# Attention and mixture of experts in one kernel: each put of rows waits for the one two in front of it

## The chip, the cores and the metric

The kernel runs on one core of a Trainium2 chip. The metric is the device time of one execution in microseconds (us); the time of the kernel before is the median of three executions. Beside these there is one profiled execution, from which all the timelines, waits and chains in this document come. PE is the matrix engine, DVE the vector engine, ACT the scalar engine, POOL the GpSimd engine; SP is the engine that issues most DMA transfers.

## The reference

The input is 16 sequences of 256 tokens with 128 channels, in float32. Four residual blocks follow each other; each one normalises its input first.

```python
x = x + attn_a(layernorm(x))   # 16 heads of 8, softmax inside blocks of 64 tokens of a sequence
x = x + ffn(layernorm(x))
x = x + attn_b(layernorm(x))   # over the axis of 16 sequences, 16 heads of 8, with a fixed bias
x = x + ffn(layernorm(x))      # the same weights as the first ffn

def ffn(x):                    # 4096 tokens, 8 experts, hidden size 512
    logits = x @ Wr
    top_vals, top_idx = top_k(logits, 2)
    rw = softmax(top_vals)
    combine = sum(rw[..., None] * one_hot(top_idx, 8), axis=1)
    h = silu(einsum('nc,ech->neh', x, Wg)) * einsum('nc,ech->neh', x, Wu)
    eo = einsum('neh,ehc->nec', h, Wd) / sqrt(12)
    return einsum('ne,nec->nc', combine, eo)
```

Each token needs only its two chosen experts, so the kernel computes only those: 8192 pairs of token and expert.

## The kernel before

The tokens are cut into four quarters `q` of 1024 tokens (64 positions of every sequence), and a quarter is held in SBUF as `xq[q]`, eight groups `g` of 128 tokens. There are two layers, `layer` 0 (attention a, then experts) and `layer` 1 (attention b, then experts).

**Attention.** `attention_a` (L397) and `attention_b` (L487) are generators that go through half a quarter in steps. In attention a, POOL adds each group's result to `xq` (L449, read here as the attention add). `layernorm_t` (L266) uses POOL for the power -1/2 (L279, the tiles `rs`), and `add_row` (L309) adds a bias row on POOL.

**Routing.** `router(layer, q)` (L585) normalises a quarter, computes the logits on PE, picks two experts for every token on DVE, and works out for each pair the row of a large table in DRAM, `sorted_in[layer]`, in which the rows of each expert lie together. It then puts the rows there: for each of the 8 groups and both choices one indirect DMA on POOL's queue (L694) takes 128 rows of 132 numbers from the tile `row` and writes each to its own place `pos_i`. That is 16 puts for a quarter, 128 in both layers. Each has to follow a DVE instruction named `beat`, the last of the attention or expert step issued beside it. The tile `row` is one of two buffers; a copy (L605) into it marks its next use.

**Experts.** `experts(layer)` (L852) goes through 39 tiles of 256 sorted rows. Which tile belongs to which expert is read from tables that `tile_tables` (L710) computes on DVE in three lists of 9, 8 and 22 tiles: the first list may start when the rows of two quarters are in place, the second after the third quarter, the last after the fourth. `fetch` (L853) issues four DMAs on SP's queue: the tile's rows `xin` (L861), which has to wait for all puts of rows that its list knows of, and the expert's three weights (L877 to L879). There are three buffers for each, so a tile is fetched two tiles ahead. PE turns the rows (`xt`, L889), computes `g` and `u` (L947) and, through `th` and `h` on ACT and DVE, `acc` (L897) and the turned result `y` (L908); ACT weighs it into `yo` (L913), DVE computes the places `to` (L918), and POOL puts the 256 result rows by two indirect DMAs (L920) into `results[layer]`: 156 puts in both layers. `y` and `to` have six buffers each.

**Combining.** `combine` (L969) reads result rows back on SP's queue (L973), after all puts of those tiles that may hold them (`READY`), and adds them to `xq`. In layer 1 the sum goes out.

**What sets the order.** The loops at the end weave generators: routing of one quarter and units of expert tiles run beside the attention of the next quarter. The Tile framework then schedules instructions on each engine's queue by its own estimate of when each can start, and sets semaphore waits for the dependences. [...] Puts into one table don't order each other, because they are declared members of a group without dependences:

```python
tc.declare_no_dep(put_row.ins, group=key, reason="rows of different places")
tc.add_to_no_dep_group(key, put_row.ins)
follow(put_row.ins, before[layer] + beat)
```

`follow` adds a dependence by hand. The framework gives the DMAs on POOL's queue eight completion semaphores in turn, so a put waits for the one eight in front of it before.

Of the kernel before, what the change touches and what calls it, by code (L numbers as in the profile page):

```python
# [110 lines left out]
def hybrid_kernel(  # L111
# [19 lines left out]
    nc = tc.nc  # L131
# [85 lines left out]
    rows = [const.tile([P, NG, TOP, RW], F32, name=f"rows{i}") for i in range(2)]  # L217
# [8 lines left out]
    sorted_in = [dram.tile([NE * NTOK, RW], F32, name=f"sorted_in{i}") for i in range(2)]  # L226
    results = [dram.tile([TOP * NTOK + KMAX * TT, C], F32, name=f"results{i}") for i in range(2)]
# [15 lines left out]
    before, after, puts = {}, {}, {}  # L243
# [3 lines left out]
    def follow(ins, others):  # L247
        for other in others:
            tc.add_manual_dep(ins, other.name, SYNC, reason="rows by places read at run time")
# [2 lines left out]

    beat, att_last = [None], [None]
    arrived = [None]


    def behind_now(put):
# [327 lines left out]
    def router(layer, q):  # L585
        n = f"F{layer}_{q}"
        row = rows[q % 2]
# [88 lines left out]
        place = p1.tile([P, NG, NE], F32, tag="place", name=f"place_{n}")  # L676
# [14 lines left out]
        key = f"rows_{layer}"  # L691
        for g in range(NG):
            for k in range(TOP):
                put_row = nc.gpsimd.indirect_dma_start(  # L694
                    out=sorted_in[layer],
                    out_offset=bass.IndirectOffsetOnAxis(ap=pos_i[:, k, g : g + 1], axis=0),
                    in_=row[:, g, k, :], in_offset=None,
                )
                tc.declare_no_dep(put_row.ins, group=key, reason="rows of different places")
                tc.add_to_no_dep_group(key, put_row.ins)  # L700
                follow(put_row.ins, before[layer] + beat)
                after.setdefault((layer, q), []).append(put_row.ins)
                yield
            if next(listing, listing) is None:
                yield
# [146 lines left out]
    def experts(layer):  # L852
        def fetch(li, i):  # L853
            n = f"{layer}_{li}_{i}"
            t = p3.tile([P, 2, RW], F32, tag="xin", name=f"xin_{n}")
            tab_i, behind = tables[layer, li]
            row = nc.values_load(
                tab_i[0:1, 1, i : i + 1], engines=[SP], min_val=0, max_val=NE * NTOK - TT,
                skip_runtime_bounds_check_because="no tile is behind the last expert's region",
            )  # L860
            got = nc.sync.dma_start(  # L861
                out=t.rearrange("p b r -> p (b r)"),
                in_=sorted_in[layer][bass.ds(row, TT)].rearrange("(p b) r -> p (b r)", b=2),
            )
            known = [put for q in range(LISTED + li) for put in after[layer, q]]
            key = f"rows_{layer}"
            tc.declare_no_dep(
                got.ins, group=key, keep=known, reason="rows that the list did not know"
            )
            tc.add_to_no_dep_group(key, got.ins)  # L870
            follow(got.ins, known)
            e = nc.values_load(
                tab_i[0:1, 0, i : i + 1], engines=[SP], min_val=0, max_val=NE - 1,
                skip_runtime_bounds_check_because="a count of at most NE - 1 experts",
            )
            w = p3.tile([P, 3, HID], F32, tag="w", name=f"w_{n}")
            nc.sync.dma_start(out=w[:, 0], in_=wg[bass.ds(e, 1)].rearrange("e c h -> (e c) h"))  # L877
            nc.sync.dma_start(out=w[:, 1], in_=wu[bass.ds(e, 1)].rearrange("e c h -> (e c) h"))
            nc.sync.dma_start(  # L879
                out=w[:, 2].rearrange("p (n c) -> p n c", c=C),  # L880
                in_=wd[bass.ds(e, 1)].rearrange("e (n p) c -> p (e n) c", p=P),
            )
            return t, w, no_pads if behind is None else behind[:, i]

        def turned(li, i, t):
            s = f"{layer}_{li}"
            pt = psum(f"xt_{s}_{i}")
            for b in range(2):
                nc.tensor.transpose(pt[:, b * P : (b + 1) * P], t[:, b, 0:C], ident)  # L889
            xT = p2.tile([P, TT], F32, tag="xT", name=f"xT_{s}_{i}")  # L890
            nc.scalar.copy(xT, pt[:, 0:TT])
            return xT

        def down(li, i, t, w, elsewhere, acc, pair, h):
            for j in range(2):
                hc = 2 * pair + j
                nc.tensor.matmul(  # L897
                    acc[:, 0:TT], lhsT=w[:, 2, hc * P : (hc + 1) * P],
                    rhs=h[:, j * TT : (j + 1) * TT],
                    start=(hc == 0), stop=(hc == NHC - 1),  # L900
                )
            if pair == 1:
                n = f"{layer}_{li}_{i}"
                yT = p2.tile([P, TT], F32, tag="yT", name=f"yT_{n}")
                nc.scalar.copy(yT, acc[:, 0:TT])  # L905
                py = psum(f"y_{n}")
                for b in range(2):
                    nc.tensor.transpose(  # L908
                        py[:, b * P : (b + 1) * P], yT[:, b * P : (b + 1) * P], ident
                    )  # L910
                y = p6.tile([P, 2, C], F32, tag="y", name=f"yo_{n}")
                for b in range(2):
                    nc.scalar.activation(  # L913
                        y[:, b, :], py[:, b * P : (b + 1) * P], AF.Identity,
                        scale=t[:, b, C : C + 1],
                    )
                to = p6.tile([P, 2], I32, tag="to", name=f"to_{n}")
                nc.vector.tensor_tensor(to, t[:, :, C + 1], elsewhere, ALU.max)  # L918
                for b in range(2):
                    put_row = nc.gpsimd.indirect_dma_start(  # L920
                        out=results[layer],
                        out_offset=bass.IndirectOffsetOnAxis(
                            ap=to[:, b : b + 1], axis=0
                        ),
                        in_=y[:, b, :], in_offset=None,
                    )
                    key = f"result_{layer}"
                    tc.declare_no_dep(put_row.ins, group=key, reason="rows of different places")
                    tc.add_to_no_dep_group(key, put_row.ins)
                    puts.setdefault(layer, []).append(put_row.ins)  # L930

        todo = [(li, i) for li, k in enumerate(LISTS) for i in range(k)]
        fetched = [fetch(*todo[0]), fetch(*todo[1])]
        xT = turned(*todo[0], fetched[0][0])
        pending = None
        for at, (li, i) in enumerate(todo):
            t, w, elsewhere = fetched.pop(0)
            s = f"{layer}_{li}"
            acc = ps_acc.tile([P, 512], F32, tag="acc", name=f"acc_{s}_{i}")
            for pair in range(2):  # L940
                m = f"{s}_{i}_{pair}"
                pg = ps_gu.tile([P, CH], F32, tag="gu", name=f"g_{m}")
                pu = ps_gu.tile([P, CH], F32, tag="gu", name=f"u_{m}")
                for k, p in ((0, pg), (1, pu)):
                    for j in range(2):
                        hs = slice((2 * pair + j) * P, (2 * pair + j + 1) * P)
                        nc.tensor.matmul(  # L947
                            p[:, j * TT : (j + 1) * TT], lhsT=w[:, k, hs], rhs=xT,
                            start=True, stop=True,
                        )  # L950
                th = p2.tile([P, CH], F32, tag="th", name=f"th_{m}")
                nc.scalar.activation(th, pg, AF.Tanh, scale=0.5)  # L952
                nc.vector.scalar_tensor_tensor(th, th, 1.0, pg, ALU.add, ALU.mult)  # L953
                h = p3.tile([P, CH], F32, tag="h", name=f"h_{m}")
                beat[0] = nc.vector.tensor_tensor(h, th, pu, ALU.mult).ins  # L955
                if pending is not None:
                    down(*pending)
                pending = (li, i, t, w, elsewhere, acc, pair, h)
                if pair == 0 and at + 2 < len(todo):
                    fetched.append(fetch(*todo[at + 2]))  # L960
                if pair == 0 and at + 1 < len(todo):
                    xT_next = turned(*todo[at + 1], fetched[0][0])
                yield
            xT = xT_next
        down(*pending)
        yield
# [167 lines left out]
```

## Time and profile before

| What | Value |
|---|---|
| timed executions | 983.7 us median of 3 (980.76 to 985.01) |
| the profiled execution, its own time | 1056.63 us |
| its span, first to last instruction | 1054.9 us |
| mean granted clock of PE | 0.911 |
| POOL busy | 361.1 us (34%), 404 instructions |
| of these, puts of rows (L694) | 128, 125.0 us, 977 ns each |
| of these, puts of results (L920) | 156, 154.1 us, 988 ns each |
| DMA queue of POOL | 18.89 MB, 5.1% of the 16 DMA engines' span |
| DMA queue of SP and ACT, dynamic | 87.36 MB, 27.8% |

The profile lists, for each engine, the busy time of groups of equal instructions and the idle time just before them with what ended it. The chain that ended last is followed back from the last instruction, at each step to what released it; its shares add up to the span. "issue" is time in which nothing that the profile shows was waited for, and "another core or an unknown queue" is a wait whose releaser it doesn't find. The busy time of a put on POOL is the writing of its descriptors. In answers in order of time a line gives the start, the duration, the engine, the line, the operation with output and inputs, and in brackets the idle time before it with its releaser.

### The profile page before, as it was taken

To read this page: it belongs to the slowest core of one execution; us is meant where nothing else is said; L and a number is where in the kernel's file an instruction comes from. 1 tells how busy PE (TensorE), PEld (TensorE's weight loads), DVE (VectorE), ACT (ScalarE), POOL (GpSimd) and SP (SyncE) were. 2 spreads that over 40 slices of the span, in tenths; PEclk is the share of its full clock that TensorE was granted. 3 is DMA by queue.
4 is the path that set the end of the run, shared out by engine and by line. 5 is a ranking of instruction groups with operands and counts; after the bars stand their busy time and mean duration, and the time that the engine had idled before them with its cause. 6 is when DMAs were issued, how large, how long until landed. Compare 5 with 4: busy or idle time off the path is not lost.

```text
span 1054.9 us, 17640 instructions
## 1 busy us (share of the span) xinstructions
PE 901.1 (85%) x5992; PEld 733.6 (70%) x5992; DVE 619.6 (59%) x1749; ACT 397.6 (38%) x773; POOL 361.1 (34%) x404
## 2 busy tenths in 40 slices
PE   5987897989989979989887789588976997999993
PEld 3765666768778758877765667467765776887872
DVE  4676357557746745577766447546754674456452
ACT  2442243244434323436444254233622332443431
POOL 2121522442443463341112631442225345333322
PEclk9997787689989999999997889898978988999997
DMA  7000000041333545673121211133203444568772
GB/s 198 3 2 1 29 14 1 21 127 41 99 101 106 151 149 166 196 225 96 42 81 41 65 58 42 61 95 127 81 14 109 121 134 148 170 192 253 222 213 88
DMA packets 104922, 107.69 MB, mean 102 GB/s; under 512 B 10688, under 2 KB 80320, under 8 KB 104832
## 3 DMA queue, kind: packets, MB, share of 16 engines
q1 hardware_dynamic: 95024, 87.36, 27.8%
q0 software_dynamic: 9088, 18.89, 5.1%
q8 instruction: 48, 0.79, 0.3%
q10 hardware_dynamic: 720, 0.30, 0.1%
q14 instruction: 42, 0.34, 0.1%
HBM read 83.38 MB, written 23.13 MB: 101 GB/s over the span
## 4 chain that ended last, share of the span: by engine, by line
PE 66%; DVE 12%; DMA 6%; another core or an unknown queue 5%; ACT 5%; issue 4%; POOL 1%; SPq 1%; ACTq 0%; POOLq 0%; DVEq 0%
PE g L947 11%; PE acc L897 10%; PE u L947 10%; PE o_A L441 6%; PE sc_A L411 6%; PE t_A L430 3%; PE v_B L354 3%; PE o_B L554 2%; DMA back<-results 2%; PE sc_B L517 2%; DMA xin<-sorted_in 2%; DMA results<-yo,to 2%; PE v_A L354 2%; PE lg_F L599 1%
## 5 line engine op out<-in xcount | busy, mean ns | idle before, releaser
L920 POOL DMA_INDIRECT results<-yo,to x156 | 154.1, 988 | 299.7 <-ACT yo L913 269.3
L897 PE MATMUL acc<-h,w 128*128 128x256 f32 x624 | 174.3, 401 | 12.1 <-DVE h L955 9.1
L947 PE MATMUL g<-xT,w 128*128 128x256 f32 x624 | 171.5, 394 | 4.4 <-issue 2.7
L947 PE MATMUL u<-xT,w 128*128 128x256 f32 x624 | 169.8, 393 | 3.8 <-DVE th L953 2.0
L952 ACT ACTIVATE th<-g 128x512 f32<-128x512 f32 x156 | 93.6, 600 | 203.8 <-PE g L947 132.1
L953 DVE SCALAR_TENSOR_TENSOR th<-th,g 128x512 f32<-128x512 f32 x156 | 106.4, 683 | 105.6 <-ACT th L952 84.0
L694 POOL DMA_INDIRECT sorted_in<-rows,pos_i_F x128 | 125.0, 977 | 124.7 <-issue 38.4
L897 PEld LDWEIGHTS acc<-h,w 128*128 128x128 f32 x624 | 121.6, 200 | 36.4 <-DVE h L955 14.8
L947 PEld LDWEIGHTS g<-xT,w 128*128 128x128 f32 x624 | 119.0, 198 | 23.0 <-issue 4.9
L947 PEld LDWEIGHTS u<-xT,w 128*128 128x128 f32 x624 | 115.7, 196 | 20.4 <-issue 3.4
L955 DVE TENSOR_TENSOR h<-th,u 128x512 f32<-128x512 f32 x156 | 106.6, 684 | 21.6 <-remote 5.6
L411 PE MATMUL sc_A<-k_A,q_A 128*128 128x256 f32 x256 | 86.4, 456 | 19.0 <-DVE ex_A L420 14.1
L441 PEld LDWEIGHTS o_A<-va,eT_A 128*64 128x64 f32 x1024 | 63.6, 147 | 20.4 <-issue 8.4
L411 PEld LDWEIGHTS sc_A<-k_A,q_A 128*128 128x128 f32 x256 | 50.8, 225 | 33.2 <-DVE ex_A L420 16.3
L441 PE MATMUL o_A<-va,eT_A 128*64 128x18 f32 x1024 | 67.7, 219 | 5.6 <-issue 3.1
L905 ACT COPY yT<-acc 128x256 f32<-128x256 f32 x78 | 29.0, 372 | 100.6 <-PE acc L897 89.2
L419 DVE TENSOR_REDUCE mx_A<-sc_A 128x8 f32<-128x512 f32 x64 | 43.1, 681 | 35.5 <-PE sc_A L411 34.8
L434 ACT COPY eT_A<-t_A 128x512 f32<-128x512 f32 x64 | 36.6, 589 | 67.9 <-PE t_A L430 61.8
L449 POOL TENSOR_TENSOR xq<-xq,att_A 128x128 f32<-128x128 f32 x32 | 14.6, 456 | 130.5 <-DVE att_A L373 120.1
L913 ACT ACTIVATE yo<-y,xin 128x128 f32<-128x128 f32 x156 | 48.6, 366 | 20.4 <-PE y L908 10.6
L425 ACT ACTIVATE ex_A<-ex_A 128x1024 f32<-128x1024 f32 x32 | 34.0, 1064 | 42.5 <-DVE ex_A L420 31.0
L430 PEld LDWEIGHTS t_A<-k_sb,ex_A 128*128 128x128 f32 x256 | 34.0, 159 | 20.7 <-issue 10.4
(173 smaller groups left out, 1318.0 us busy)
## 6 DMA issues: line engine op xcount, KB each, us to landing
w<-in_wg SPq DMA_DIRECT2D x78, 256.0 KB
w<-in_wu SPq DMA_DIRECT2D x78, 256.0 KB
w<-in_wd SPq DMA_DIRECT2D x78, 256.0 KB
xin<-sorted_in SPq DMA_DIRECT2D x78, 132.0 KB
back<-results SPq DMA_DIRECT2D x16, 512.0 KB
results<-yo,to POOLq DMA_INDIRECT x156
sorted_in<-zero SPq DMA_DIRECT2D x2, 1056.0 KB
sorted_in<-rows,pos_i_F POOLq DMA_INDIRECT x128
```

The source lines that it names most:

```text
L354: nc.tensor.matmul(pv[:, a * P : (a + 1) * P], lhsT=src[:, g * n + a].rearrange("p r k -> p (r k)"), rhs=w, start=True, stop=True,)
L411: nc.tensor.matmul(sc[:, v * 4 * BS : (v + 1) * 4 * BS], lhsT=qT[:, blk, 2 * v : 2 * v + 2, :].rearrange("p r k -> p (r k)"), rhs=kx[:, :, ...
L430: nc.tensor.transpose(pt[:, i * P : (i + 1) * P], ex[:, b, 2 * i : 2 * i + 2, :].rearrange("p h k -> p (h k)"), ident,)
L441: nc.tensor.matmul(po[b * BS : (b + 1) * BS, i * 18 : (i + 1) * 18], lhsT=eT[:, b, 2 * v + i % 2, u * BS : (u + 1) * BS], rhs=vt[:, b, 2 * ...
L694: put_row = nc.gpsimd.indirect_dma_start(out=sorted_in[layer], out_offset=bass.IndirectOffsetOnAxis(ap=pos_i[:, k, g : g + 1], axis=0), in ...
L897: nc.tensor.matmul(acc[:, 0:TT], lhsT=w[:, 2, hc * P : (hc + 1) * P], rhs=h[:, j * TT : (j + 1) * TT], start=(hc == 0), stop=(hc == NHC - 1),)
L913: nc.scalar.activation(y[:, b, :], py[:, b * P : (b + 1) * P], AF.Identity, scale=t[:, b, C : C + 1],)
L920: put_row = nc.gpsimd.indirect_dma_start(out=results[layer], out_offset=bass.IndirectOffsetOnAxis(ap=to[:, b : b + 1], axis=0), in_=y[:, b ...
L947: nc.tensor.matmul(p[:, j * TT : (j + 1) * TT], lhsT=w[:, k, hs], rhs=xT, start=True, stop=True,)
L952: nc.scalar.activation(th, pg, AF.Tanh, scale=0.5)
L953: nc.vector.scalar_tensor_tensor(th, th, 1.0, pg, ALU.add, ALU.mult)
L955: beat[0] = nc.vector.tensor_tensor(h, th, pu, ALU.mult).ins
```

## The change

A new function `put_rows` issues every put of rows, for the experts' rows and for the results. It keeps a list `flight` of all puts in the order of the program. A put has to follow the last but one entry of that list, that is, the put two in front of it, in whichever table that one wrote. As a dependence on a DMA is on its completion, the put is not issued before that one has landed. The other dependences are unchanged.

```diff
+    flight = []
+
+    def put_rows(out, place, src, key, others=()):
+        put = nc.gpsimd.indirect_dma_start(
+            out=out, out_offset=bass.IndirectOffsetOnAxis(ap=place, axis=0), in_=src,
+            in_offset=None,
+        ).ins
+        tc.declare_no_dep(
+            put, group=key, keep=flight[-2:-1], reason="rows of different places"
+        )
+        tc.add_to_no_dep_group(key, put)
+        follow(put, flight[-2:-1] + list(others))
+        flight.append(put)
+        return put
...
-                put_row = nc.gpsimd.indirect_dma_start(
-                    out=sorted_in[layer],
-                    out_offset=bass.IndirectOffsetOnAxis(ap=pos_i[:, k, g : g + 1], axis=0),
-                    in_=row[:, g, k, :], in_offset=None,
+                put = put_rows(
+                    sorted_in[layer], pos_i[:, k, g : g + 1], row[:, g, k, :], key,
+                    before[layer] + beat,
                 )
-                tc.declare_no_dep(put_row.ins, group=key, reason="rows of different places")
-                tc.add_to_no_dep_group(key, put_row.ins)
-                follow(put_row.ins, before[layer] + beat)
-                after.setdefault((layer, q), []).append(put_row.ins)
+                after.setdefault((layer, q), []).append(put)
...
-                    put_row = nc.gpsimd.indirect_dma_start(
-                        out=results[layer],
-                        out_offset=bass.IndirectOffsetOnAxis(
-                            ap=to[:, b : b + 1], axis=0
-                        ),
-                        in_=y[:, b, :], in_offset=None,
+                    puts.setdefault(layer, []).append(
+                        put_rows(
+                            results[layer], to[:, b : b + 1], y[:, b, :], f"result_{layer}"
+                        )
                     )
-                    key = f"result_{layer}"
-                    tc.declare_no_dep(put_row.ins, group=key, reason="rows of different places")
-                    tc.add_to_no_dep_group(key, put_row.ins)
-                    puts.setdefault(layer, []).append(put_row.ins)
```

The scheduler knows of the new dependences. In the changed program the order on ACT's queue is the same; on POOL many puts of rows stand behind attention adds, `rs` or results that they preceded; on PE, DVE and SP a few instructions move, most of them around the start of layer 1's experts: DVE's first `to` conversions go behind the last attention step, and SP's read of the last results goes ahead of part of the second tile's and all of the third tile's fetch.

## The prediction

> **What bounds the kernel now.** I read the page first: its header, the chain that ended last and the two groups of puts.
>
> ```profile
> span 1054.9 us, 17640 instructions
> PE 901.1 (85%) x5992; PEld 733.6 (70%) x5992; DVE 619.6 (59%) x1749; ACT 397.6 (38%) x773; POOL 361.1 (34%) x404
> ...
> PE 66%; DVE 12%; DMA 6%; another core or an unknown queue 5%; ACT 5%; issue 4%; POOL 1%; SPq 1%; ACTq 0%; POOLq 0%; DVEq 0%
> ...
> L920 POOL DMA_INDIRECT results<-yo,to x156 | 154.1, 988 | 299.7 <-ACT yo L913 269.3
> ...
> L694 POOL DMA_INDIRECT sorted_in<-rows,pos_i_F x128 | 125.0, 977 | 124.7 <-issue 38.4
> ```
>
> PE sets the pace (66% of the chain), POOL hardly appears (1%). The 284 puts (156 + 128) fill 279 us of POOL's 361. Result puts mostly wait for ACT's `yo`; row puts wait for little. So a wait on a put costs time only if it outlasts POOL's idle time and somebody then misses the rows.
>
> Second, SP's own waits, for who needs the rows:
>
> ```profile
> SPq L861 <- DMA sorted_in<-rows,pos_i_F: 38.0, 3, 28.1
> SPq L973 <- DMA results<-yo,to: 27.4, 7, 13.7
> ```
>
> Only 3 tile fetches and 7 reads of results waited for a put.
>
> Third, POOL in order of time, at the end of the fourth quarter's routing in layer 0:
>
> ```profile
> 382.23 0.96 POOL L920 DMA_INDIRECT results<-yo,to  x1 [2.48 <-ACT yo L913]
> 383.49 0.96 POOL L920 DMA_INDIRECT results<-yo,to  x1 [0.30 <-issue]
> 384.76 0.96 POOL L694 DMA_INDIRECT sorted_in<-rows,pos_i_F  x1 [0.30 <-issue]
> ...
> 391.08 0.96 POOL L920 DMA_INDIRECT results<-yo,to  x1 [0.30 <-issue]
> ```
>
> Queued puts start 0.96 + 0.30 = 1.26 to 1.27 us apart, so two of them take 2.53.
>
> Fourth, the chain in order of time, in layer 1:
>
> ```profile
> 586.56 8.34 another core or an unknown queue
> 604.25 5.49 another core or an unknown queue
> ...
> 1041.12 2.24 DMA results<-yo,to
> ```
>
> The first two lie inside unbroken runs of puts (583.35 to 593.17, 602.48 to 608.58): PE had issued its matmuls, but DVE and ACT saw them done only when the run was over. The last is the final put, landing 2.24 us after its start.
>
> **The Trainium skill.** "DMA: Bandwidth & Descriptors", section "Anatomy of one DMA — SWDGE (gpsimd) path", gives such a DMA about 2.0 us fixed plus bytes/436e3, and says that a semaphore wait happens on the issuing sequencer. For 128 rows of 528 B that is 2.0 + 0.155, an estimate of 2.16 us; the trace has 2.28 in quiet stages, in fair agreement. "Perfetto Trace Analysis", section "DMA Instruction — SWDGE (GPSIMD)", says that the profiled end is the end of writing descriptors, not of the data: the trace agrees, 0.96 us on POOL against 2.28 to landing. The wait must be set against the 2.28.
>
> **The change part by part.** Landings come from the trace's semaphore events (where 15 or 16 of the 16 are recorded): row puts 2.26 at the least, median 2.29; result puts median 3.45, at most 5.7. Where events are missing I take the last packet and add 0.39 (2.28 against 1.89 where both are known). From a landing to the waiting POOL instruction is 0.15 us (138.14 to 138.29).
>
> (a) The wait in quiet stages. Put n would start 2.53 us after put n-2; it may start 2.28 + 0.15 = 2.43 after it. The condition is met 0.1 us early: nothing. That covers all 32 row puts of the first two quarters of layer 0 and most of layer 1's first three. In the pure expert stages result pairs come 5.62 us apart (409.07, 414.69), and each put's forerunner is the same half of the previous pair; against 3.45 + 0.15 nothing again, bar single ones beside reads of results (454.18, landing 5.8 later), which hold POOL 2 us with nothing urgent behind. The tail's last puts stand 3.8 us behind their forerunners, which land in 2.2: nothing.
>
> (b) The wait in mixed stages, the fourth quarter of each layer, where weights stream: mean landing 2.95, so (2.95 + 0.15)/2 = 1.55 per put instead of 1.27 when queued. Queued behind a waiting put are other puts, the row-table copy (L605), and for whoever follows, `rs` and the added attention. For layer 0 I redo the end in the new order, which puts the last two rows behind the results of tile 1_4. Starts, each the later of 1.27 after the last and (landing of n-2) + 0.15: rows 385.0, 387.2, 388.5, 389.9; results 391.2, 393.2; rows 394.2, 396.9, the last landing at about 400.1 (landings used: 2.63, 3.50, 3.38, 2.55, 2.57, 3.15, 2.85, 3.50, 3.2). The first fetch of the last list, at 395.82 before, goes to 400.25, +4.4. It landed 2.1 us after issue (397.9) and PE first used it at 402.34: now it lands at 402.35. Cost 0, cover used up. Layer 1 likewise: two rows at 885.3 and 886.5, two at 891.1 and 892.4 (held by DVE as before), results 895.0 and 896.3, rows 898.1 and 899.4, landing 902.6; fetch 902.75 instead of 898.38; in SBUF 904.95 instead of 900.58; used at 902.87. PE waits 2.1 us. The first weights follow in step.
>
> (c) The order. Tile's scheduler sees the waits and puts rows behind `xq` adds. In layer 0's second quarter five rows now stand behind the sixth attention add (218.40): last row 225.4 instead of 220.36, first fetch 227.9 instead of 223.13. PE first uses it at 237.36, so nearly 10 us of cover hide 4.8; without them it would cost those 4.8. In layer 1's second quarter eight rows instead of four follow the results ready at 692.13: last row near 703.6 instead of 701.1, fetch 706.6 instead of 704.06, landed about 710; PE uses it at 716.40. Hidden.
>
> (d) Layer boundary. On DVE two `to` conversions leave their place ahead of `att_B`; there PE waited 3.33 us (to 712.04) behind DVE's `to`, which waited for a fetch. That goes, but PE next waits at `lnp_B` (727.85) for the read of results that SP issues at 714.66, when the last put has landed, as before. One u pair (0.87 us) moves ahead of that wait and fills it: -0.9, at most -3.1. SP takes this read before the second tile's `wd` and the third tile; they go out about 6 us later (the third tile's rows near 717 instead of 711.14) and are first used at 725.56: nothing.
>
> Sum: 0 + 2.1 - 0.9 = +1.2 us on the profiled execution of 1056.63 us (span 1054.9 and 1.7 around it). The timed median is 983.7, so 73 us of the profiled execution are not in the timed ones; I carry the 1.2 over unscaled: **985**, own range 980 to 990.
>
> What the trace of before doesn't show is whether the held completions of the fourth view are in timed runs. The chain puts about 51 us on them. Both ends stay in the range: there fully, or not at all.
>
> **Rivals.** *Slower: POOL becomes the bound of the fourth quarters.* If the held completions belong to the profiled execution alone, PE's part of those stages shrinks (gaps of 2.4, 2.8 and 2.6 us in layer 0's) and POOL's 26 queued puts set the time: 26 x (1.55 - 1.27) = 7.3 us per layer, 14.6, less the covers of 4.4 and 2.3: +8, **992**. It decides from the point where the last row lands less than the fetch's 2.1 us before PE needs the tile; with landings of 3.4 throughout it is 26 x (1.775 - 1.27) = 13 per layer, +19, 1003. For it speaks the 73 us; against, that POOL idles 2.5 to 4.5 us three times in these stretches.
>
> *Faster: fewer held completions.* They ended 0.3 to 1.7 us after a run of puts paused. In layer 1's first quarter `rs_B`, waiting for DVE, now stands behind four rows instead of twelve, so the run ends at 588.1 and not 593.2: about 5 us. Where landings exceed 2.4 us the wait itself opens pauses, up to 1 us each. A quarter of 51 us gives -12, **972**; half gives 958. Against it: the longest two (8.34, and 7.7 at 673) lie in quiet stages where (a) leaves the spacing alone, and each needed a pause that the wait doesn't make.
>
> *The change does nothing on the chip:* the landing is always there first. Then only the order counts: 983 to 985, not told apart from my forecast.
>
> **Chances.** Forecast and nothing together 0.40; POOL-bound 0.30, and 0.04 for a wait in front of `rs` or an `xq` add that reaches PE; fewer held completions 0.26. About 0.5% (5 us) is what a measurement of this kernel tells from no change. So faster 0.26, same 0.40, slower 0.34. Leaving out the lower part of the faster case and the upper end of the slower one gives 972 to 998.
>
> **What would show it.** Right: row puts at 1.27 us in the quarters with quiet DMA; 1.5 to 1.6 in the fourth ones; the first fetch of the last list about 4 us nearer to PE's use; no PE gap for `xin` at the first list. Wrong: POOL puts 2 us or more apart in quiet runs (wake-up dearer than 0.15); the "unknown queue" share well under 5%; a new PE gap before the first tiles; `rs` waiting behind puts.

## The result, and the profile after

The changed kernel takes **1023.6 us** (median; 1020.7 to 1025.66) against 984.4 (median of four) for the kernel before: 1.039 times as long, with a 95% interval of 1.033 to 1.045. The prediction had said 985 with a range of 972 to 998. It was wrong. Medians in this document are over all executions of a kernel, while ratios and their intervals leave out slow ones (over 1.5% above the fastest of the same kernel), among them 13 of 20 of the kernel "own table" and 5 of 20 of "fourth quarters free" below, both with the profiled one.

The page of the changed kernel; the columns are those of the page before:

```profile
span 1018.9 us, 17633 instructions
PE 876.1 (86%) x5992; PEld 719.6 (71%) x5992; DVE 619.3 (61%) x1749; ACT 396.5 (39%) x773; POOL 357.8 (35%) x404
...
PE 66%; DMA 12%; DVE 9%; issue 4%; ACT 4%; POOL 3%; SPq 1%; ACTq 0%; POOLq 0%; DVEq 0%
...
L260 POOL DMA_INDIRECT results<-yo,to x156 | 151.3, 970 | 321.1 <-ACT yo L925 242.0
...
L260 POOL DMA_INDIRECT sorted_in<-rows,pos_i_F x128 | 124.5, 973 | 122.9 <-DMA sorted_in<-rows,pos_i_F 28.1
...
L901 PE MATMUL xt<-k_sb,xin 128*128 128x128 f32 x156 | 31.9, 287 | 54.6 <-DMA xin<-sorted_in 45.7
```

Three things differ from before. DMA has gone from 6% of the chain to 12%, and "another core or an unknown queue", 5% before, is no longer there. The idle time ahead of row puts is ended most often by the landing of a row put (28.1 of 122.9 us; before it was "issue", 38.4 of 124.7). And PE now idles 54.6 us in front of `xt`, of which 45.7 end with the arrival of a tile's rows. SP's own waits agree:

```profile
SPq L873 <- DMA sorted_in<-rows,pos_i_F: 106.8, 13, 31.3
SPq L979 <- DMA results<-yo,to: 28.2, 7, 13.0
```

13 tile fetches now wait for a put of rows (106.8 us), where the prediction's profile had 3 (38.0 us); the reads of results are as they were.

PE's instructions in order of time show where its idle time lies. The three lines are the first tile of the last list in layer 0, of the first list in layer 1 and of the last list in layer 1; the bracket is the idle time before:

```profile
388.56 0.69 PE L901 MATMUL xt<-k_sb,xin 128*128 128x128 f32 x2 [14.30 <-DMA xin<-sorted_in]
...
682.24 0.66 PE L901 MATMUL xt<-k_sb,xin 128*128 128x128 f32 x2 [8.46 <-DMA xin<-sorted_in]
...
865.40 0.69 PE L901 MATMUL xt<-k_sb,xin 128*128 128x128 f32 x2 [16.17 <-DMA xin<-sorted_in]
```

Together that is 38.9 us, which looks like the whole loss of 39. It is not so simple, as the experiments show.

The chain in order of time, ahead of the first of these lines, shows how a put passes the delay on. Columns: start, duration, what.

```profile
376.45 2.26 DMA sorted_in<-rows,pos_i_F
378.70 0.02 issue
...
378.75 0.72 issue
379.46 0.56 POOL results L260
...
383.73 2.28 DMA sorted_in<-rows,pos_i_F
...
386.38 2.13 DMA xin<-sorted_in
388.51 0.04 issue
388.56 0.69 PE xt L901 x2
```

The put of 376.45 lands in 2.26 us, the next but one starts 0.75 us later, and so on; the last row lands at 386.01, SP fetches at once, and PE starts when the fetch is in. There is no cover left anywhere: put, landing, put, landing, fetch, PE.

### The profile page after: what moved, and what is told of

It is laid out like the page before. It is cut to its first block, busy times and chain, and to the rows that moved or that the text cites. A ratio compares the mean times of both kernels' runs of the same rounds, so it can differ in the third digit from the quotient of the medians.

```text
span 1018.9 us, 17633 instructions
## 1 busy us (share of the span) xinstructions
PE 876.1 (86%) x5992; PEld 719.6 (71%) x5992; DVE 619.3 (61%) x1749; ACT 396.5 (39%) x773; POOL 357.8 (35%) x404
## 4 chain that ended last, share of the span: by engine, by line
PE 66%; DMA 12%; DVE 9%; issue 4%; ACT 4%; POOL 3%; SPq 1%; ACTq 0%; POOLq 0%; DVEq 0%
PE g L953 11%; PE u L953 10%; PE acc L909 10%; PE o_A L457 6%; PE sc_A L427 6%; DMA sorted_in<-rows,pos_i_F 5%; PE t_A L446 3%; PE o_B L570 2%; DMA back<-results 2%; DMA results<-yo,to 2%; DMA xin<-sorted_in 2%; PE v_B L370 2%; PE sc_B L533 2%; PE v_A L370 2%; PE lg_F L615 2%
## 5 line engine op out<-in xcount | busy, mean ns | idle before, releaser
L260 POOL DMA_INDIRECT results<-yo,to x156 | 151.3, 970 | 321.1 <-ACT yo L925 242.0
L909 PE MATMUL acc<-h,w 128*128 128x256 f32 x624 | 168.6, 391 | 1.8 <-DVE h L961 1.4
L260 POOL DMA_INDIRECT sorted_in<-rows,pos_i_F x128 | 124.5, 973 | 122.9 <-DMA sorted_in<-rows,pos_i_F 28.1
L959 DVE SCALAR_TENSOR_TENSOR th<-th,g 128x512 f32<-128x512 f32 x156 | 106.3, 682 | 85.3 <-ACT th L958 83.9
L909 PEld LDWEIGHTS acc<-h,w 128*128 128x128 f32 x624 | 118.8, 195 | 23.3 <-DVE h L961 5.9
L427 PE MATMUL sc_A<-k_A,q_A 128*128 128x256 f32 x256 | 83.6, 443 | 17.9 <-DVE ex_A L436 12.5
L901 PE MATMUL xt<-k_sb,xin 128*128 128x128 f32 x156 | 31.9, 287 | 54.6 <-DMA xin<-sorted_in 45.7
L901 PEld LDWEIGHTS xt<-k_sb,xin 128*128 128x128 f32 x156 | 19.4, 146 | 59.4 <-DMA xin<-sorted_in 38.1
L903 ACT COPY xT<-xt 128x256 f32<-128x256 f32 x78 | 29.5, 379 | 55.3 <-PE xt L901 55.2
```

The costliest lines, as they stand in the source:

```text
L260: put = nc.gpsimd.indirect_dma_start(out=out, out_offset=bass.IndirectOffsetOnAxis(ap=place, axis=0), in_=src, in_offset=None,).ins
L427: nc.tensor.matmul(sc[:, v * 4 * BS : (v + 1) * 4 * BS], lhsT=qT[:, blk, 2 * v : 2 * v + 2, :].rearrange("p r k -> p (r k)"), rhs=kx[:, :, ...
L909: nc.tensor.matmul(acc[:, 0:TT], lhsT=w[:, 2, hc * P : (hc + 1) * P], rhs=h[:, j * TT : (j + 1) * TT], start=(hc == 0), stop=(hc == NHC - 1),)
```

## The experiments

All times below are medians, with the ratio to the kernel before on the same chip and its 95% interval. The diffs are against the changed kernel and are cut (`...`): `keep` of `declare_no_dep` changes along with the wait and is left out. Two theories stood against each other at first. **Cadence**: with two puts in flight, a pair of puts takes a landing plus a wake-up; in the fourth quarters POOL has no idle time to pay for that, the last rows go out late, and PE waits. **Order**: the new dependences make the scheduler keep rows behind results whose `yo` is late, and the wait itself is harmless.

### The order alone, two per table, four in front, one in front

```diff
 order_only
-        follow(put, flight[-2:-1] + list(others))
+        follow(put, list(others))
+        for other in flight[-2:-1]:
+            tc.add_manual_dep(put, other.name, ORDER, reason="order alone")
 own_table
-    flight = []
+    flights = {"rows": [], "result": []}
...
+        flight = flights[key.split("_")[0]]
 d4
-        follow(put, flight[-2:-1] + list(others))
+        follow(put, flight[-4:-3] + list(others))
 d1
-        follow(put, flight[-2:-1] + list(others))
+        follow(put, flight[-1:][:1] + list(others))
```

`ORDER` is a dependence without a semaphore: it places instructions and makes none wait.

> The puts keep nearly the order of the changed kernel (in both fourth quarters exactly: rows and results alternate as the program has them), but no put waits for another to land. Theory 'cadence' (two puts in flight: a pair of puts takes one landing plus one wake-up, 3.0 us where DMA is quiet and the put has a second wait, about 4.3 beside weights, against 2.53 before): no cost, 984 within 5 us. Theory 'order' (a row put now stands behind result puts whose yo is late, so the last rows go out late whatever the wait): about 1020, with PE gaps of 8 to 16 us ahead of the first tiles of the lists.

> Each put waits for the one two in front of it in its own table, so up to four are in flight where rows and results alternate; the order of the fourth quarters is again that of the kernel before, and each put still carries its extra wait. Cadence: four in flight need (3.7 + 0.8)/4 = 1.1 us per put, less than the 1.27 of queued puts, so 984 to 990. Order: 984. If the extra wait instruction itself were the cost (0.5 us on each put, met or not): near 1010.

> Each put waits for the one four in front, across tables as in the changed kernel; PE, DVE, ACT and SP have the order of the kernel before. Cadence: as own_table, 984 within 5. Cross-table waits as such (a row that can't go before the yo of a result in front of it) would still cost: above 995. For the profiled execution: if five or more puts in flight are what holds PE's completions back, the share of unknown queues goes and its time falls from 1056 to the timed one; if it needs more than that, nothing.

> Each put waits for the one right in front. Cadence: 2.3 + 0.3 to 0.8 in quiet stages, 3.5 to 4.5 beside weights; about 25 puts between the tables of two quarters cost another 25 x (4.3 - 2.15) = 54 us less the slack of quiet stages, in each of three lists: 1130 to 1200. Order: same order as the changed kernel within two places, so about 1020 plus at most 10.

Measured: order alone 992.8 us (1.011, 1.005 to 1.017); own table 988.4 (1.002, 0.998 to 1.006); four in front 998.5 (1.015, 1.010 to 1.021); one in front 1272.1 (1.295, 1.286 to 1.305).

The order theory falls as the main cause: with the changed kernel's order of the fourth quarters and no wait, PE idles only a little ahead of the last lists. The kernel with the order alone, PE in order of time, layers 0 and 1:

```profile
380.73 0.44 PE L904 MATMUL xt<-k_sb,xin 128*128 128x128 f32 x2 [2.42 <-DMA xin<-sorted_in]
...
834.54 0.44 PE L904 MATMUL xt<-k_sb,xin 128*128 128x128 f32 x2 [2.30 <-DMA xin<-sorted_in]
```

The order is not free, though: two result puts now stand ahead of the last row, and 992.8 is 1.1% above the kernel before. The two gaps explain about 3.6 us of it (2.42 + 2.30, less the 1.16 which a second profile of the kernel before has in layer 1, below). PE is also busy for 3.4 us longer (869.2 us against 865.8 in that profile). The rest stays open.

Cadence has the sign right everywhere, and two sizes wrong. One put in flight costs 290 us, not 150 to 220. PE's gaps ahead of the six lists make 153 us (47.6 and 45.1 ahead of the last ones), about what was expected. What the expectation lacked is that PE also idles some 100 us more at other places (57 behind DVE's `th`, 40 for the rows of later tiles) and is busy 31 us longer. Four in front was to be free and costs 16 us.

Own table came out in its range, but not because its puts are as quick as expected: they take 1.46 and 1.58 us each (table below), and PE waits 2.9, 5.4 and, at the first list of layer 1, 6.3 us for rows. Against that, it lacks most of PE's waits for `lnp_B` and `ot_B` early in layer 1 (3.1 us where the second profile of the kernel before has 19.0; these waits come up again below).

One more thing shows in these profiles: the kernel with the order alone was profiled at 991.03 us, as fast as its timed executions, though no put in it waits for any nearer than eight in front. So unbroken runs of puts don't by themselves cause the held completions that the prediction saw.

### The kernel before, profiled once more

> The kernel before, unchanged, for a second profiled execution. If holding back PE's completions belongs to the kernel whenever it is profiled: about 1056 again, with 5% on unknown queues. If it was a trait of that one execution (the kernel with the order alone was profiled at 991 with no wait added): 980 to 990, POOL's puts of both fourth quarters in one unbroken run at 1.27 us, and the first fetch of the last list at the moment when PE needs it, within 3 us.

Measured: 983.2 us, and the profiled execution 983.89. So the 1056.63 us of the profile that the prediction rests on, with its 51 us on an unknown queue, did not come again: none of the other profiles here has a share on an unknown queue. The page of the second one:

```profile
span 982.1 us, 17640 instructions
...
PE 865.8 (88%) x5992; PEld 713.3 (73%) x5992; DVE 621.2 (63%) x1749; ACT 397.1 (40%) x773; POOL 359.1 (37%) x404
...
L920 POOL DMA_INDIRECT results<-yo,to x156 | 152.3, 976 | 269.1 <-ACT yo L913 237.1
...
L694 POOL DMA_INDIRECT sorted_in<-rows,pos_i_F x128 | 125.0, 976 | 99.5 <-issue 33.5
```

PE is busy for 865.8 us instead of 901.1, and 11 fetches wait for row puts (55.5 us in all), not 3. More important is the end of layer 0's fourth quarter in order of time:

```profile
366.61 0.96 POOL L694 DMA_INDIRECT sorted_in<-rows,pos_i_F  x1 [0.30 <-DMA sorted_in<-rows,pos_i_F]
367.87 0.96 POOL L694 DMA_INDIRECT sorted_in<-rows,pos_i_F  x1 [0.30 <-issue]
369.13 0.96 POOL L694 DMA_INDIRECT sorted_in<-rows,pos_i_F  x1 [0.31 <-issue]
370.40 0.96 POOL L694 DMA_INDIRECT sorted_in<-rows,pos_i_F  x1 [0.30 <-DMA sorted_in<-rows,pos_i_F]
...
372.94 0.33 SPq L861 DMA_DIRECT2D xin<-sorted_in  x1
...
376.13 0.38 PE L889 MATMUL xt<-k_sb,xin 128*128 128x128 f32 x2
```

POOL issues a put every 1.27 us here, with no pause, and the whole quarter looks like this: from the first row (340.84) to the last (370.40) 23 puts follow, 1.29 us each. The fetch goes out when the last row has landed; with 2.13 us, as the fetch of the changed kernel took, it is in at about 375.1, 1.0 us before PE takes it. In layer 1 the fetch goes out at 827.07, and PE waits 1.16 us for it. So **POOL had no pause left in either fourth quarter, and the rows came with 1.0 us of cover in one and none in the other.** In the disturbed profile the same two stretches took 1.54 and 1.68 us per put, POOL idled in them, and PE came 4.4 and 2.3 us after its rows.

The same stretches in the changed kernel take 25 puts of 1.80 and 1.88 us. Layer 0's is 44.9 us long instead of 29.6: 15.4 later, less 1.0 of cover, is 14.4, and the gap is 14.3.

### Where the wait costs: the fourth quarters freed, and the fourth quarters only

```diff
 fourths_free
+    FREE = {*range(66, 92), *range(208, 234)}
...
+        ahead = [] if len(flight) in FREE else flight[-2:-1]
...
-        follow(put, flight[-2:-1] + list(others))
+        follow(put, ahead + list(others))
 lists_free
+    FREE = {*range(66, 92), *range(146, 170), *range(208, 234)}
 fourths_only
+    HELD = {*range(66, 92), *range(208, 234)}
...
+        ahead = flight[-2:-1] if len(flight) in HELD else []
```

> The wait is left out for the 26 puts between the first row and the last row of each layer's fourth quarter (rows and results), and stays for the other 232. If the wait costs because POOL bounds these two stretches: the gaps of 14.3 and 16.2 us go, 993 (988 to 998), and the one of 8.4 us at the first list of layer 1 stays. If it costs all along the kernel, in quiet stages too: above 1005.

> As the fourth quarters free, and also the 24 puts that go with the second quarter's rows of layer 1. POOL-bound theory: the gap of 8.4 us goes too, 985 (980 to 990), though over 200 puts still wait. Cost all along: above 1005.

> The wait only for the 26 puts of each fourth quarter; all others as in the kernel before. POOL-bound theory: the two gaps of 14 to 16 us ahead of the last lists come back, and each is followed by 4 to 6 us at half the PE clock (about 2.3 us each); the gap of 10.5 us ahead of lnp_B at the start of layer 1, which the kernel before has and the changed one hasn't, stays. So it is slower than the changed kernel although it waits less: 983 + 14.3 + 16.2 + 4.6 - 1 = 1017 (1010 to 1025). If the loss needs waits elsewhere too: below 1005.

Measured: fourth quarters free 985.0 us (1.003, 1.000 to 1.005); with layer 1's second quarter free as well 980.4 (0.997, 0.994 to 1.001); fourth quarters only 1013.3 (1.032, 1.027 to 1.037). So 52 of 284 puts carry nearly the whole loss: without their wait it is gone, and their wait alone makes 32 of the 39 us. This includes the order: without the wait, the fourth quarters have the order of the kernel before (23 puts from the first row to the last), with it that of the changed one (25), and the order alone cost 11 us. PE in order of time with the wait in the fourth quarters only:

```profile
386.00 0.69 PE L903 MATMUL xt<-k_sb,xin 128*128 128x128 f32 x2 [14.36 <-DMA xin<-sorted_in]
...
855.68 0.69 PE L903 MATMUL xt<-k_sb,xin 128*128 128x128 f32 x2 [15.00 <-DMA xin<-sorted_in]
```

Both gaps are back. Freeing the fourth quarters came out 8 us better than expected, although the gap at the first list of layer 1 stayed, as foreseen (8.15 us before the `xt` at 664.85). What offsets it is a gain elsewhere, which the expectation for the last experiment below takes up: the kernel before has a gap of 10.5 us shortly ahead of that list, and neither the changed kernel nor this one has it.

### Distance on the queue

In the kernel with four in front, the scheduler had moved pairs of results ahead of pairs of rows, so that four in front in the program was sometimes only two in front on POOL's queue (its put at 368.99 waits for the landing of a result put from 363.70, with three puts between them in the program but only one on the queue). Two kernels keep the order of the changed kernel in the fourth quarters and wait for the put four or three in front.

```diff
 d4_in_order (d3_in_order has flight[-3:-2])
-        follow(put, flight[-2:-1] + list(others))
+        follow(put, flight[-4:-3] + list(others))
+        for other in flight[-2:-1]:
+            tc.add_manual_dep(put, other.name, ORDER, reason="order alone")
```

> Each put waits for the one four in front, and the order of the fourth quarters is that of the changed kernel, so that four in front in the program is also four in front on POOL's queue. If d4 cost 16 us because the scheduler had moved result puts ahead, so that the put waited for stood only two or three in front on the queue: the gaps of 6 us ahead of the last lists go, 984 to 993 (the order alone had 993). If waiting for a put of the other table costs as such: about 998 with the same gaps.

> Each put waits for the one three in front, in the changed kernel's order of the fourth quarters. With landings of 2.9 there and a wake-up of 0.8 for a put with two waits, three in flight make (2.9 + 0.8)/3 = 1.23 us per put, just under the 1.27 of POOL itself: 990 to 997, as with the order alone (993) and at distance four in order (994). If every wait that is met late costs POOL more than that: 1.4 us per put and gaps of 3 to 5 us ahead of the last lists, 1000 to 1006.

Measured: four in order 994.1 us (1.013, 1.010 to 1.015), three in order 999.4 (1.019, 1.014 to 1.024). Four in order costs no more than the order alone, so the cross-table wait as such is not the cost; its profiled execution, though, was the fastest of six (984.0), so its gaps below may be small ones. Three in order missed the range of its first expectation; the second, 1.4 us per put and gaps of 3 to 5 us, comes nearer. The table sets all of them side by side: time per put from the first to the last row of the fourth quarters, and PE's gap ahead of the first tile of the last lists.

| Kernel | per put, layers 0 and 1, us | PE gap, us | time, us |
|---|---|---|---|
| before, second profile | 1.29, 1.33 | none, 1.2 | 983.2 |
| fourth quarters free | 1.28, 1.33 | none, 1.1 | 985.0 |
| order alone | 1.32, 1.32 | 2.4, 2.3 | 992.8 |
| four in order | 1.32, 1.39 | 2.2, 3.9 | 994.1 |
| three in order | 1.45, 1.52 | 5.5, 7.1 | 999.4 |
| own table | 1.46, 1.58 | 2.9, 5.4 | 988.4 |
| four in front | 1.60, 1.60 | 6.1, 5.8 | 998.5 |
| two in front, fourth quarters only | 1.80, 1.83 | 14.4, 15.0 | 1013.3 |
| two in front (the change) | 1.80, 1.88 | 14.3, 16.2 | 1023.6 |
| one in front | 3.05, 3.18 | 47.6, 45.1 | 1272.1 |

The gap follows the time per put. For two in flight the mean fits: landings of 2.83 us on average and a wake-up (the time from the landing to the start of the waiting put) of 0.77 make (2.83 + 0.77)/2 = 1.80. For three, (3.12 + 0.77)/3 = 1.30 does not: it took 1.45 and 1.52. Landings there spread from 2.2 to 5.3 us, and a put held by a late one can't be made up, since in no profile here do two puts start less than 1.26 us apart. That is the likely reason; it was not tested apart.

### A version that beats both

In the second profile of the kernel before, POOL, DVE and PE early in layer 1, in order of time:

```profile
571.59 0.95 POOL L694 DMA_INDIRECT sorted_in<-rows,pos_i_F  x1 [0.30 <-issue]
572.56 1.06 POOL L279 TENSOR_TENSOR rs_B<-ve_B,minus_half 128x4 f32<-128x4 f32 x1
...
579.99 1.04 POOL L279 TENSOR_TENSOR rs_B<-ve_B,minus_half 128x4 f32<-128x4 f32 x1
581.07 2.94 DVE L286 TENSOR_SCALAR ln_B<-xq,mv_B,rs_B 128x128 f32<-128x128 f32 x4 [6.13 <-POOL rs_B L279]
...
584.75 0.47 PE L299 MATMUL lnp_B<-k_sb,ln_B 128*128 128x128 f32 x1 [10.51 <-DVE vb L360]
```

The first `rs_B` stands behind 12 row puts without a pause and the second behind five more puts; DVE waits 6.13 us for it, and PE 10.5 for DVE. In the changed kernel the first stands behind 4, as the prediction had read from the new order, and PE waits 2.6. So the next kernel keeps the wait for these puts alone.

```diff
 first_b_only
+    HELD = {*range(128, 146)}
...
+        ahead = flight[-2:-1] if len(flight) in HELD else []
```

> The wait only for the 18 puts from the first row of layer 1 on (both runs of rows that stand beside rs_B on POOL). In the kernel before, rs_B stands behind an unbroken run of 16 puts and PE waits 10.5 us for it; here it moves ahead of most of them. If that gap is worth its length: 973 (970 to 978), faster than both kernels. If PE only arrives earlier at the next wait (the first list of layer 1, or DVE's attention): 980 to 984.

Measured: **969.4 us** (0.987, 0.983 to 0.991), faster than both, if only by 1.3% than the kernel before, and below the expected range by 0.6. The same place in its profile:

```profile
565.74 0.98 POOL L262 DMA_INDIRECT sorted_in<-rows,pos_i_F  x1 [1.69 <-DMA sorted_in<-rows,pos_i_F]
566.74 1.04 POOL L297 TENSOR_TENSOR rs_B<-ve_B,minus_half 128x4 f32<-128x4 f32 x1
...
571.49 0.65 PE L317 MATMUL lnp_B<-k_sb,ln_B 128*128 128x128 f32 x4 [0.25 <-ACT lnB L475]
```

The second `rs_B` still stands behind five puts of rows, one of which waits 1.69 us, but the first comes earlier, and PE's gap is gone; the first list of layer 1 is in time all the same. Whether the new place of `rs_B` does it alone, without the waits, was not tried.

## Why the prediction was wrong, point by point

**The basis.** "I carry the 1.2 over unscaled", said the prediction, from a profiled execution 73 us longer than the timed ones. It named the doubt but took from that profile what decided it: the idle time of POOL in the fourth quarters and the moment when PE wants the rows. Why that one execution was longer is not known; one further profile of the same kernel was not, and neither the order nor the wait is needed for that.

**(a) Quiet stages, "nothing": right in layer 0, not in layer 1.** In layer 0's second quarter four row puts stand 1.27 us apart (216.80 to 220.61). There the wake-up is about 0.26, so 2.27 + 0.26 = 2.53, exactly the two put slots. But in the first three quarters of layer 1 a put takes 1.81, 1.73 and 1.69 us from the first row to the last, against 1.41, 1.28 and 1.28 both in the second profile of the kernel before and with the order alone. So the wait does cost POOL time there. It reaches PE at one place, the first list of layer 1, see (c).

**(b) The fourth quarters, "0" and "2.1 us": the step that failed.** They cost PE 14.3 and 16.2 us. Each quarter can be counted from its first row. The profile of the kernel before has the first rows, and PE's first use of the last list's first tile, in layers 0 and 1 at

```profile
353.07 0.96 POOL L694 DMA_INDIRECT sorted_in<-rows,pos_i_F  x1 [1.67 <-DVE pos_i_F L687]
402.34 0.38 PE L889 MATMUL xt<-k_sb,xin 128*128 128x128 f32 x2
...
853.76 0.96 POOL L694 DMA_INDIRECT sorted_in<-rows,pos_i_F  x1 [1.57 <-DVE pos_i_F L687]
902.87 0.38 PE L889 MATMUL xt<-k_sb,xin 128*128 128x128 f32 x2
```

and the changed kernel has its first rows at

```profile
338.80 0.96 POOL L260 DMA_INDIRECT sorted_in<-rows,pos_i_F  x1 [1.67 <-DVE pos_i_F L703]
...
813.78 0.96 POOL L260 DMA_INDIRECT sorted_in<-rows,pos_i_F  x1 [1.57 <-DVE pos_i_F L703]
```

| us after the quarter's first row, layers 0 and 1 | forecast | measured |
|---|---|---|
| last row put | 43.8, 45.6 | 44.9, 47.1 |
| first tile of the last list in SBUF | 49.3, 51.2 | 49.7, 51.6 |
| PE has done all that comes before this tile | 49.3, 49.1 | 35.5, 35.5 |

The rows came within 0.4 us of the forecast. PE was there 13.8 and 13.7 us earlier, and that is nearly the whole of both gaps. So the term that failed is the cover: "PE first used it at 402.34" and "used at 902.87" were read from that one execution. In the second profile of the kernel before PE is there after 35.3 and 35.5 us, as in the changed kernel.

That the rows were timed well was luck, since two errors cancel. The idle time of POOL in that profile stayed in the forecast (its quarters took 35.5 and 38.6 us from the first row to the last, those of the second profile 29.6 and 30.6), and the wake-up was too short. The 0.15 had been read at a copy (L605, started at 138.29), not at a put. The landing was not mis-sized (2.95 said, 2.83 measured). The Trainium skill, "Perfetto Trace Analysis", section "Identifying Dependency Chains", says that an instruction waiting on multiple engines may get EventSemaphore instructions ahead of it for the further conditions; so it is here, and the trace prices it. Where the put itself carries the wait for the landing it starts a median of 0.27 us after it (29 late puts of the changed kernel); where such an instruction ahead of it does, 0.77 (73 late puts). With one put in flight the two are 0.27 (84) and 0.76 (178). The chain shown above has 0.75.

How much is whose can be estimated. With the true cover and the 1.55 per put of the prediction, the last row would start 25 x 1.55 = 38.8 us after the first, and with the 4.8 us that the changed kernel takes from there to SBUF (383.73 to 388.51) PE would wait 38.8 + 4.8 - 35.5 = 8 us. The other 6 us of layer 0's gap are the longer time per put, 25 x (1.80 - 1.55): the dearer wake-up, (0.77 - 0.15)/2 = 0.31 us per put, less 0.06 for the landings.

**(c) The order, "hidden": half right.** Layer 0's first list is in time. Layer 1's has a gap of 8.46 us, which was not foreseen. Counted from the first row of layer 1, the last row of its second quarter is put after 106.3 us, much as in the second profile of the kernel before (105.7), but PE is there after 102.9 us instead of 120.8, since its waits of 10.5 us for `lnp_B` and 8.5 for `ot_B` are gone but for 2.6. So PE gained, and the rows, held by the wait, did not: with the second quarter of layer 1 free as well, the last row is put after 97.8 us and the gap is gone. With the fourth quarters free, the kernel that has this gap and the one before differ by only 2 us.

**(d) The layer boundary, "-0.9":** too small for these runs to show.

**The rivals.** "POOL becomes the bound of the fourth quarters" was the right mechanism, with the right reason ("if the held completions belong to the profiled execution alone"). Its price of +8, at most +19, rested on the same covers (4.4 and 2.3, where the second profile has 1.0 and none) and the same wake-up; and it counted as many puts as before, where the new order has two more in each of these stretches. "Fewer held completions" found its place by accident: `rs_B` behind four rows instead of twelve does save PE about 8 us (10.5 to 2.6), but because PE waits for `rs_B`, not through completions.

**The balance.** The spans of the two undisturbed profiles differ by 36.8 us. PE's busy time grew by 10.3 (865.8 to 876.1) and its idle time by 26.5 (116.3 to 142.8, span less busy). The idle time is +14.3 and +15.0 at the last lists, +8.5 at the first list of layer 1, -7.9 at `lnp_B` (10.5 to 2.6) and -8.5 at `ot_B` (6.18 and 2.35, both gone); smaller changes of both signs make the rest. Why PE is busy longer with the same 5992 matmuls is in part explained in the last section.

## What to carry to other kernels

Before pricing a wait, find the stretches in which the issuing engine's queue is already full; there a longer interval is paid in full, times the number of entries, and a few dozen puts out of hundreds can carry the whole loss. Count a wait that stands on an instruction of its own ahead of a put as dearer than one that the put carries (0.77 against 0.27 us here), and count the distance on the queue, not in the program. A profile whose own time is 7% off the timed median is no basis for a cover of a few microseconds, and a position in it that comes out right can still be two errors that cancel. A cap on puts in flight can help where a short instruction that the critical engine needs stands behind a long run of them.

## What was not expected of the hardware

PE slows down after each of the three new gaps: after the one of 8.46 us, too, the granted clock is 0.50 for 4 us (682.3 to 686.3). The changed kernel by stretches around layer 0's gap and after it; PEclk is the granted clock, the columns before it are busy time and instructions:

```profile
374.30:388.50 14.20, 0.00 (x0) 0.00 (x0) 0.00 (x0) 0.89 (x3) 8.91 (x12) 0.68 0.18 55
388.50:392.50 4.00, 3.94 (x11) 3.23 (x12) 1.45 (x3) 0.37 (x1) 1.91 (x2) 0.50 0.99 312
392.50:396.50 4.00, 4.00 (x20) 3.48 (x19) 1.54 (x3) 1.06 (x3) 0.00 (x0) 0.93 0.49 158
396.50:400.50 4.00, 4.00 (x21) 3.56 (x20) 1.96 (x4) 1.88 (x5) 1.91 (x2) 1.00 0.40 98
```

For the first 4 us after the gap the clock is 0.50 and PE does 11 matmuls instead of some 21; then it is back. At 0.50 and 0.93 that loses 4 x 0.50 + 4 x 0.07 = 2.3 us; after layer 1's gap (0.50, then 0.81) 2.8. The Trainium skill, "TensorE: Matmul & The Clock Gate", Part 1, says that the array's clock falls to half after an idle window of about 3.4 us and comes back after one that is busy, and the trace agrees. In the second profile of the kernel before, the clock is 1.00 throughout this stretch (340 to 395). So each of these two gaps, of 14.3 and 16.2 us, costs 2 to 3 us more than its length: together about 5 of the 10.3 us by which PE's busy time grew. The rest is not accounted for here.
